# Attention scores by phases of three pairs of banks, with whole projections in between

## The chip, the cores and the metric

The kernel runs on one core of a Trainium2 chip. The metric is the device time of one execution in microseconds (us). A core has five engines that run their own instruction streams and meet through semaphores: TensorE (PE in the profile, its weight loads PEld), VectorE (DVE), ScalarE (ACT), GpSimd (POOL) and SyncE (SP, which here only issues DMAs). Matmul results lie in PSUM, which has eight banks of 128 partitions by 512 f32.

## The reference

A decoder layer over four sequences (B = 4) of 1024 tokens with 512 features, all in f32, with 16 heads of 32:

```
x = x + attn(layernorm(x))              # gated self-attention
x = x + xattn(layernorm(x), ctx)        # cross-attention, keys and values from ctx (384 features)
x = x + ffn(layernorm(x))               # 64 small networks with 16 hidden units each

attn:  a = softmax(inner @ outer.T / sqrt(32)) * aperture[q] * expression[k]
       a = a / (a.sum(-1) + 1e-8);  out = rotate(a @ v) @ Wout
xattn: out = softmax(q @ k.T / sqrt(32)) @ v @ Wo + bo
```

The two gates are sigmoids of small projections of x. The rotation of the heads is folded into the output weights.

## The kernel before, in words

**Units.** A unit is one of the two blocks (`ph` 0: self-attention, the first block; `ph` 1: cross-attention and the networks, the second) for one sequence; `order` has eight of them, first block first. Each unit has two halves (`hf`) of 512 queries. `attention(u, hf)` makes the list of 32 steps of a half unit: four groups `g` of four heads, and in each group eight key tiles `kt` of 128 keys.

**A step.** `scores(g, kt)` (L597 to L630) computes the scores of four heads, keys on partitions, queries on columns. It does so in two pairs `i` of two heads `j`. Each pair has a tile `s` of two PSUM banks, from a pool of two such tiles. Head `2 * i + j` has its queries and keys on 32 partitions of its own, so its matmul uses 32 rows of the array, and 64 of its columns (L608):

```
r = slice((2 * i + j) * DH, (2 * i + j + 1) * DH)
for m in range(0, P, 64):
    nc.tensor.matmul(s[m : m + 64, j, :],
        lhsT=k[r, g, kt * P + m : kt * P + m + 64], rhs=q[r, g, :], ...)
```

ScalarE takes the exponential of a pair in one instruction of 128x1024 (L613) into a tile `e`; six such tiles rotate. The denominators need sums of `e` over all keys. VectorE adds up the tiles of a pair in `es` (L619 at the second key tile, L621 after), for both pairs in most of the second block, and for the first pair alone where `shared` is set (the first block and the last unit); there the second pair's sums are made by TensorE (L643). In the first block VectorE also sums the first pair times the expression gate in `eg` (L628 for the first product, L629 for the rest). `es` and `eg` have tiles of their own.

**Times values.** `finish` of a step is held in `late` and issued one step later, after that step's scores. It multiplies `e` with the values into the accumulator `av` (L635), four heads side by side in four column tiles of 128 rows by 32 columns. At the last key tile `normalize` copies `av` and `sm` (L652, L654), and `after(steps, f)` puts the rest off by so many steps: `add_up` sums `es` and `eg` over partitions (L665) and sends the sums through DRAM (SyncE), `divide` forms reciprocals (L702), `multiply` makes the normalized result over the queries (L715).

**What goes beside.** `beside(u, hf)` lists all other work of a half unit in order: layernorm, transposes and projections of the unit to come (`pre`), and output projection, residual, layernorm and networks of the half before (`post`). Each part carries a load; a projection has three or four parts of load 1, each of which issues four column matmuls with `columns` (L87) over one chunk of 128 features. `run` hands parts out after every step in proportion to the load, so a projection can be spread over some steps while its bank stays open. `bank()` gives these banks, from a pool of two; another two hold `av` and `sm`. With the four banks of `s` that makes eight. Banks are emptied by ScalarE in most cases (`evacuate`, L281 and L283), by VectorE for values of the first block (L537) and for the output projections (L804).

**Order.** All engines' instructions stay in the order in which the program writes them. There is no planner; the order above is all there is.

**Roots.** A layernorm takes mean and variance on VectorE, then `rsqrt` (L289 to L301) on VectorE: an integer estimate and three Newton steps, twelve instructions on 128x4, and then `normalized` (L304). Only the very first half tile has its roots on GpSimd, as an addition and a power with the column `power` of -0.5 (L406, L407). GpSimd otherwise adds a bias (L812), copies marks (L829) and issues a few DMAs.

Of the kernel before, what the change touches and what calls it, by code (L numbers as in the profile page):

```python
# [16 lines left out]
P = 128  # L17
# [46 lines left out]
def moderate_path(tc: tile.TileContext, a: dict, out: bass.AP, flag: bass.AP):  # L64
    nc = tc.nc
    x = a["x"]
    with ExitStack() as st:
# [10 lines left out]
        p4 = enter(tc.tile_pool(name="mp4", bufs=4))  # L78

        def bank():  # L80
            return pf.tile([P, HALF], F32, tag="f", name="f")

        def columns(to, lhsT, rhs, **flags):
# [205 lines left out]
        def rsqrt(mv, n):  # L289
            ve = p2.tile([P, n], F32, tag="ve", name="ve")  # L290
            nc.vector.tensor_scalar(ve, mv[:, :, 1], EPS, None, ALU.add)
            yi = p2.tile([P, n], I32, tag="yi", name="yi")
            nc.vector.tensor_scalar(yi, ve.bitcast(I32), 1, None, ALU.logical_shift_right)
            nc.vector.tensor_scalar(yi, yi, -1.0, float(MAGIC), ALU.mult, ALU.add)
            y = yi.bitcast(F32)
            w = p2.tile([P, n], F32, tag="nw", name="nw")
            for _ in range(3):
                nc.vector.scalar_tensor_tensor(w, y, -0.5, y, ALU.mult, ALU.mult)
                nc.vector.tensor_tensor(w, w, ve, ALU.mult)
                nc.vector.scalar_tensor_tensor(y, w, 1.5, y, ALU.add, ALU.mult)  # L300
            return y  # L301
# [55 lines left out]
        def pre(u):  # L357
# [87 lines left out]
            def proj(what, g, hf):  # L445
# [3 lines left out]
                def part(cs):  # L449
                    def f():  # L450
                        if cs[0] == 0:
                            if "w" + what not in me:
                                fetch(what)
                            me["pj"] = bank()
                        for c in cs:
                            columns(
                                me["pj"], me["w" + what][:, c, ts(g, P)], me[kind, hf](c),
                                start=(c == 0), stop=(c == n - 1),
                            )
                        if cs[-1] == n - 1:  # L460
                            copy(me["pj"])
                    return len(cs), f
# [51 lines left out]
            def values(kt):  # L514
# [5 lines left out]
                def part(cs):  # L520
                    def f():
                        if cs[0] == 0:
                            if kt == 0:
                                if "wv" not in me:
                                    fetch("v")
                                me["v"] = p2.tile([P, NT, H, DH], F32, tag="v", name="v")
                            me["pv"] = bank()
                        for c in cs:
                            columns(
                                me["pv"], me[kind, hf, "t"](c, t), me["wv"][:, c, :],  # L530
                                start=(c == 0), stop=(c == n - 1),
                            )
# [52 lines left out]
        def attention(u, hf):  # L585
# [13 lines left out]

            def scores(g, kt):  # L600
                q, k = me["q", hf], me["k"]
                es = []
                for i in range(2):
                    s = ps.tile([P, 2, HALF], F32, tag="s", name="s")
                    for j in range(2):
                        r = slice((2 * i + j) * DH, (2 * i + j + 1) * DH)
                        for m in range(0, P, 64):
                            nc.tensor.matmul(  # L608
                                s[m : m + 64, j, :], lhsT=k[r, g, kt * P + m : kt * P + m + 64], rhs=q[r, g, :],
                                start=True, stop=True,  # L610
                            )
                    e = p4.tile([P, 2, HALF], F32, tag="e", name="e", bufs=6)
                    nc.scalar.activation(e, s, AF.Exp, scale=SCALE)  # L613
                    es.append(e)
                me["e", kt] = es
                for i in range(1 if shared and not closing(g) else 2):
                    if kt == 1:
                        me.setdefault("es", {})[i] = p1.tile([P, 2, HALF], F32, tag=f"es{i}", name="es")
                        nc.vector.tensor_tensor(me["es"][i], me["e", 0][i], es[i], ALU.add)  # L619
                    elif kt > 1:  # L620
                        nc.vector.tensor_tensor(me["es"][i], me["es"][i], es[i], ALU.add)  # L621
                if ph == 0 and kt > 0:
                    if kt == 1:
                        me["eg"] = p1.tile([P, 2, HALF], F32, tag="es1", name="eg")
                    for h in range(2):
                        eg, gate = me["eg"][:, h, :], lambda t: me["sw"][:, t, HG * g + h, 1:2]
                        if kt == 1:
                            nc.vector.tensor_scalar(eg, me["e", 0][0][:, h, :], gate(0), None, ALU.mult)  # L628
                        nc.vector.scalar_tensor_tensor(eg, es[0][:, h, :], gate(kt), eg, ALU.mult, ALU.add)  # L629
                return es  # L630

            def times(g, kt, es):
# [6 lines left out]
                if shared and kt % 2 and not closing(g):  # L639

                    for j in range(4):
                        t, h = kt - 1 + j // 2, j % 2
                        nc.tensor.matmul(  # L643
                            sm[j * DH : j * DH + sums, :],
                            lhsT=me["sw"][:, t, HG * g + 2 + h, :] if ph == 0 else ones, rhs=me["e", t][1][:, h, :],
                            start=(kt == 1), stop=(kt == NT - 1),
                        )

            def normalize(g):
# [3 lines left out]
                if shared:  # L653
                    nc.scalar.copy(both[:, 1, :], sm)  # L654
                    added = [me["es"][0][:, 0, :], me["es"][0][:, 1, :]]
                    if ph == 0:
                        added += [me["eg"][:, 0, :], me["eg"][:, 1, :]]
                else:
                    added = [me["es"][h // 2][:, h % 2, :] for h in range(HG)]
                after(1, lambda: add_up(g, i, both, added), behind=True)  # L660
# [56 lines left out]

            def step(g, kt):
                def f():
                    issue_due(False)  # L720
                    es = scores(g, kt)
                    issue_due(True)
                    if late:
                        late.pop(0)()
                    late.append(lambda: finish(g, kt, es))
                    tick[0] += 1
                return f

            def finish(g, kt, es):
# [3 lines left out]

            for g in range(HG):
                for kt in range(NT):
                    steps.append(step(g, kt))
            return steps

        def settle(u, hf, g):
# [5 lines left out]
            def sums():  # L745
                for j in range(HG):
                    nc.tensor.matmul(
                        sm[j * DH : (j + 1) * DH, :], lhsT=ones.to_broadcast([P, DH]), rhs=me["es"][j // 2][:, j % 2, :],
                        start=True, stop=True,
# [12 lines left out]
        def post(u, hf):  # L762
# [24 lines left out]
            def project(t):  # L787
                def part(cs, to=None):
                    def f():
                        assert last or me["divided", hf] >= cs[-1]  # L790
                        if cs[0] == 0:
                            res["po"] = to() if to else bank()
                            res["po", t] = res["po"]
                        if last:
                            res["po"] = res["po", t]
# [29 lines left out]

            def root(a=0, n=4):
                if ph == 1:
                    i = 2 * NS + b * NT + 4 * hf + a
                    nc.gpsimd.tensor_copy(marks[:, i : i + n], res["mv"][:, a : a + n, 1])  # L829
                rs = rsqrt(res["mv"][:, a : a + n, :], n)  # L830
                for t in range(n):
# [134 lines left out]

        def run(main, items):

            parts = sum(items, [])
            total = sum(c for c, _ in parts)  # L970
            done = 0
            for n, f in enumerate(main):
                f()
                while parts and (done + parts[0][0] / 2 <= total * (n + 1) / len(main) or n == len(main) - 1):
                    c, f1 = parts.pop(0)
                    if f1:
                        f1()
                    done += c

        def pause(load):  # L980
# [20 lines left out]
        def beside(u, hf):  # L1001
# [3 lines left out]
            if u + 1 == n:  # L1005
                h, out = held[0]["h"], last["wo"] + last["load"]
                k = min(len(h), 6)
                if hf:
                    ending.append(post(u, 1))
                    out += ending[0]["wo"]  # L1010
                out += pause(2) + weave(h[0:k], pause(10)) + weave(h[k:], last["o"]) + held.pop()["out"]
                out += (ending[0]["load"] if hf else []) + weave(last["ln"], pause(5)) + last["xT"]
# [65 lines left out]
        first += p["v"][1][0:3] + pres[1]["tr"][0] + p["v"][1][3:]  # L1078
        run([lambda: None], first)
        for u in range(n):  # L1080
            if u == 0:
                crossing.append(True)
            for hf in range(2):
                run(attention(u, hf), beside(u, hf))
        tail = ending[0]
        sums, divide, look = settle(n - 1, 1, HG - 1)
        late.pop(0)()

# [675 lines left out]
```

## Time and profile before

| what | value |
|---|---|
| median of three runs | 2196.32 us (2192.43 to 2196.33) |
| the profiled execution | 2195.77 us |
| its span, first to last instruction | 2193.9 us |
| granted TensorE clock, mean | 0.997 |
| TensorE busy | 2168.4 us (99%), 22750 matmuls |
| VectorE busy | 1558.3 us (71%) |
| ScalarE busy | 1240.3 us (57%) |
| GpSimd busy | 85.3 us (4%) |
| DMA, mean | 74 GB/s |

The page of the profile gives busy times, the chain of work that ended last, and groups of instructions: line, engine, operation, output and inputs, shapes and count, then busy time and mean of one in ns, then the idle time before them and who ended it. Each f32 matmul of the program is two in the profile, since the array passes over the columns twice. Matmuls run side by side in tiles of the array, so their single durations (0.6 us) add up to more than their busy time. A timeline row has start, duration, engine, line, operation, tiles, shape and count, and in brackets the idle time before it with its releaser.

Before the first scores, at 99.4 us, the kernel prepares the first unit; the last scores start at 2136.3 us, and the tail after them ends at 2193.9.

### The profile page before, as it was taken

To read this page: it belongs to the slowest core of one execution; us is meant where nothing else is said; L and a number is where in the kernel's file an instruction comes from. 1 tells how busy PE (TensorE), PEld (TensorE's weight loads), DVE (VectorE), ACT (ScalarE), POOL (GpSimd) and SP (SyncE) were. 2 spreads that over 40 slices of the span, in tenths; PEclk is the share of its full clock that TensorE was granted. 3 is DMA by queue.
4 is the path that set the end of the run, shared out by engine and by line. 5 is a ranking of instruction groups with operands and counts; after the bars stand their busy time and mean duration, and the time that the engine had idled before them with its cause. 6 is when DMAs were issued, how large, how long until landed. Compare 5 with 4: busy or idle time off the path is not lost.

```text
span 2193.9 us, 53076 instructions
## 1 busy us (share of the span) xinstructions
PE 2168.4 (99%) x22750; PEld 557.5 (25%) x22750; DVE 1558.3 (71%) x2510; ACT 1240.3 (57%) x1493; POOL 85.3 (4%) x127
## 2 busy tenths in 40 slices
PE   9999999999999999999999999999999999999996
PEld 4322222222222222222222222222222222222223
DVE  4578675796757957577686676877777777856477
ACT  0155545555455554555656566675757666577673
POOL 2000000030300000000000000000000000000000
PEclk9999999999999999999999999999999999999998
DMA  6312133032330221211222132221223142203131
GB/s 170 117 47 72 56 97 105 19 89 66 101 113 19 85 66 51 84 37 42 69 85 94 41 93 65 79 82 48 68 89 108 50 103 69 81 20 85 54 89 41
DMA packets 154137, 161.72 MB, mean 74 GB/s; under 512 B 47002, under 2 KB 92698, under 8 KB 152740
## 3 DMA queue, kind: packets, MB, share of 16 engines
q1 hardware_dynamic: 149828, 156.14, 24.7%
q8 instruction: 180, 2.95, 0.6%
q0 software_dynamic: 2080, 0.98, 0.3%
q10 hardware_dynamic: 1984, 1.12, 0.2%
q14 instruction: 65, 0.53, 0.1%
HBM read 115.40 MB, written 42.74 MB: 72 GB/s over the span
## 4 chain that ended last, share of the span: by engine, by line
PE 94%; DVE 2%; ACT 1%; issue 1%; DMA 1%; SPq 0%; POOL 0%; DVEq 0%; ACTq 0%
PE f L87 36%; PE s L608 25%; PE av L635 21%; PE sm L643 6%; PE sm L665 3%; ACT e L613 1%; DVE es L621 1%; PE f L913 1%; PE f L875 1%; PE s L87 1%; DVE g L902 1%; DMA xin<-in_x 0%; PE f L483 0%; PE s L913 0%; ACT hid L896 0%
## 5 line engine op out<-in xcount | busy, mean ns | idle before, releaser
L613 ACT ACTIVATE e<-s 128x1024 f32<-128x1024 f32 x1024 | 993.7, 1022 | 709.5 <-PE s L608 511.9
L621 DVE TENSOR_TENSOR es<-es,e 128x1024 f32<-128x1024 f32 x534 | 642.4, 1227 | 266.0 <-ACT e L613 264.2
L608 PE MATMUL s<-q,k 32*64 32x512 f32 x8192 | 607.3, 613 | 2.4 <-ACT e L613 0.8
L635 PE MATMUL av<-e,v 128*32 128x512 f32 x4096 | 550.2, 603 | 0.0
L87 PE MATMUL f<-xT,w 128*32 128x512 f32 x2816 | 333.7, 592 | 0.0
L629 DVE SCALAR_TENSOR_TENSOR eg<-e,sw,eg 128x512 f32<-128x512 f32 x448 | 318.4, 746 | 2.3
L619 DVE TENSOR_TENSOR es<-e 128x1024 f32<-128x1024 f32 x89 | 106.7, 1223 | 220.3 <-ACT e L613 188.4
L608 PEld LDWEIGHTS s<-q,k 32*64 32x64 f32 x8192 | 132.8, 129 | 446.2 <-ACT e L613 241.8
L87 PE MATMUL f<-w,q 128*32 128x512 f32 x1984 | 240.3, 592 | 0.0
L635 PEld LDWEIGHTS av<-e,v 128*32 128x32 f32 x4096 | 87.9, 108 | 403.9 <-issue 401.3
L87 PEld LDWEIGHTS f<-xT,w 128*32 128x32 f32 x2816 | 92.1, 110 | 210.5 <-issue 206.0
L643 PE MATMUL sm<-e,sw 128*2 128x512 f32 x1024 | 133.3, 592 | 0.0
L87 PE MATMUL f<-w,xT 128*32 128x512 f32 x896 | 106.0, 592 | 0.6 <-DVE q L285 0.6
L87 PEld LDWEIGHTS f<-w,q 128*32 128x32 f32 x1984 | 65.5, 110 | 149.1 <-issue 142.6
L87 PE MATMUL f<-w,ctxT 128*32 128x512 f32 x768 | 92.6, 592 | 0.0
L896 ACT ACTIVATE hid<-sT,units 128x256 f32<-128x256 f32 x128 | 76.5, 605 | 28.5 <-DVE g L902 24.1
L87 PE MATMUL f<-ctxT,w 128*32 128x512 f32 x768 | 92.3, 592 | 0.0
L812 POOL TENSOR_TENSOR r<-res,bo_bc 128x512 f32<-128x512 f32 x32 | 40.9, 1278 | 1041.5 <-DVE res L804 790.9
L902 DVE SCALAR_TENSOR_TENSOR g<-hid,units,g 128x256 f32<-128x256 f32 x120 | 57.5, 479 | 14.2 <-ACT hid L896 9.1
L665 PE MATMUL sm<-es,fixed 128*1 128x512 f32 x348 | 65.0, 591 | 0.0
L804 DVE TENSOR_TENSOR res<-f,res 128x512 f32<-128x512 f32 x62 | 42.5, 685 | 14.9 <-PE f L87 11.1
L715 DVE TENSOR_TENSOR q<-both,recb 128x512 f32<-128x512 f32 x63 | 43.2, 685 | 7.0 <-DMA recb<-rec_d 7.0
(265 smaller groups left out, 1046.2 us busy)
## 6 DMA issues: line engine op xcount, KB each, us to landing
recb<-rec_d SPq DMA_DIRECT2D x252, 64.0 KB
xT<-rows_d SPq DMA_DIRECT2D x60, 256.0 KB
rows_d<-r SPq DMA_DIRECT2D x60, 256.0 KB
w<-in_xattn_Wo SPq DMA_DIRECT2D x9, 1024.0 KB
w<-wout_d SPq DMA_DIRECT2D x8, 1024.0 KB
res<-in_x SPq DMA_DIRECT2D x32, 256.0 KB
x1b_d<-r SPq DMA_DIRECT2D x32, 256.0 KB
res<-x1b_d SPq DMA_DIRECT2D x32, 256.0 KB
```

The lines of the kernel that those rows point to most:

```text
L87: nc.tensor.matmul(to[r], lhsT=lhsT[:, j, :] if len(lhsT.shape) == 3 else lhsT[:, r], rhs=rhs, **flags)
L608: nc.tensor.matmul(s[m : m + 64, j, :], lhsT=k[r, g, kt * P + m : kt * P + m + 64], rhs=q[r, g, :], start=True, stop=True,)
L613: nc.scalar.activation(e, s, AF.Exp, scale=SCALE)
L619: nc.vector.tensor_tensor(me["es"][i], me["e", 0][i], es[i], ALU.add)
L621: nc.vector.tensor_tensor(me["es"][i], me["es"][i], es[i], ALU.add)
L629: nc.vector.scalar_tensor_tensor(eg, es[0][:, h, :], gate(kt), eg, ALU.mult, ALU.add)
L635: nc.tensor.matmul(av[r, :], lhsT=me["v"][:, kt, HG * g + h, :], rhs=es[h // 2][:, h % 2, :], start=(kt == 0), stop=(kt == NT - 1),)
L643: nc.tensor.matmul(sm[j * DH : j * DH + sums, :], lhsT=me["sw"][:, t, HG * g + 2 + h, :] if ph == 0 else ones, rhs=me["e", t][1][:, h, :], ...
L665: nc.tensor.matmul(sm[j * DH : j * DH + 1, :], lhsT=ones, rhs=e, start=True, stop=True)
L715: nc.vector.tensor_tensor(me["q", hf][:, g, :], both[:, 0, :], all_, ALU.mult)
L896: nc.scalar.activation(hid, res["s"], AF.Relu, bias=units[:, 1, h : h + 1], scale=units[:, 0, h : h + 1])
L902: nc.vector.scalar_tensor_tensor(res["g"], res["hid"], units[:, 2, h - 1 : h], res["g"], ALU.mult, ALU.add)
```

## The change

**Phases.** Steps are replaced by phases. `attention` now returns all 64 pairs (group, key tile, pair) of a half unit and a function `phase(size, early)`. `run_phases` takes three pairs, or two where a projection's bank is open (`keep` counts those), and whatever is left at the end. A phase first issues the score matmuls of all its pairs. The first two in issue order get the two tiles `s`; the third gets two banks from `bank()`, the pool of the projections. Where a part with load is due behind the phase, the pairs are issued in the order second, third, first, so that the pair whose exponential comes first sits in the projection banks. The exponential of the pair in separate banks is two instructions of 128x512 instead of one of 128x1024.

**What lies between.** After the scores come the times-values of all steps whose second pair was in the phase before, and then the parts that are due. Once a projection has begun, all its parts follow before the next phase. Where the phase before held the end of one group and the first step of the next, the end is issued after the first exponential, and the rest behind the projections. The clock of `after` advances by half a step a pair.

**Tiles.** `es` and `eg` now come from the pool of the `e` tiles, which has eight instead of six places; they are kept by group.

**Engines.** The first gated product goes from VectorE to ScalarE. `rsqrt` becomes two GpSimd instructions, an addition and a power, and the copy of marks is issued after the root. Two pauses in the plan of the last unit have other lengths.

```diff
+        def keep(first, last):
+            open_[0] += bool(first) - bool(last)
...
         def rsqrt(mv, n):
-            ve = p2.tile([P, n], F32, tag="ve", name="ve")
-            nc.vector.tensor_scalar(ve, mv[:, :, 1], EPS, None, ALU.add)
...
-            for _ in range(3):
-                nc.vector.scalar_tensor_tensor(w, y, -0.5, y, ALU.mult, ALU.mult)
-                nc.vector.tensor_tensor(w, w, ve, ALU.mult)
-                nc.vector.scalar_tensor_tensor(y, w, 1.5, y, ALU.add, ALU.mult)
+            y = p2.tile([P, n], F32, tag="yi", name="rs")
+            nc.gpsimd.tensor_scalar(y, mv[:, :, 1], EPS, None, ALU.add)
+            nc.gpsimd.tensor_tensor(y, y, power.to_broadcast([P, n]), ALU.pow)
             return y
...
+            def wide():
+                return p4.tile([P, 2, HALF], F32, tag="e", name="e", bufs=8)
+
+            def exponentials(g, kt, i, two, whole):
+                e = wide()
+                if whole is not None:
+                    nc.scalar.activation(e, whole, AF.Exp, scale=SCALE)
+                else:
                     for j in range(2):
+                        nc.scalar.activation(e[:, j, :], two[j], AF.Exp, scale=SCALE)
...
                         if kt == 1:
-                            nc.vector.tensor_scalar(eg, me["e", 0][0][:, h, :], gate(0), None, ALU.mult)
+                            nc.scalar.activation(eg, e0[0][:, h, :], AF.Identity, scale=gate(0))
...
+            pairs = [(g, kt, i) for g in range(HG) for kt in range(NT) for i in range(2)]
+
+            def phase(size, early):
+
+                issue_due(False)
+                mine, pairs[:] = pairs[:size], pairs[size:]
+                front = early and size == 3
+                order_ = [1, 2, 0] if front else range(len(mine))
+                places = {}
+                for n, j in enumerate(order_):
+                    whole = ps.tile([P, 2, HALF], F32, tag="s", name="s") if n < 2 else None
+                    two = [bank(), bank()] if whole is None else [whole[:, m, :] for m in range(2)]
+                    multiply_into(*mine[j], two)
+                    places[j] = (two, whole)
+                border = len(late) > 1 and late[0][0] == NT - 1
+                for n, pair in enumerate(mine):
+                    exponentials(*pair, *places[n])
+                    add(*pair)
+                    if n == 0 and border:
+                        issue_due(True)
+                        late.pop(0)[1]()
+                issue_due(True)
+                while late and not border:
+                    late.pop(0)[1]()
...
+                tick[0] += size / 2
+                return lambda: [f() for _, f in now]
...
+            while pairs:
+                size = min(len(pairs), 2 if open_[0] else 3)
+                upto = total * (all_ - len(pairs) + size) / all_
...
+                others = phase(size, early)
+                while parts and (open_[0] or due(parts[0][0], done)):
                     c, f1 = parts.pop(0)
                     if f1:
                         f1()
                     done += c
+                others()
```

## The prediction

> **What bounds the kernel.** I read the page first (busy shares, chain, groups), then TensorE's timeline of one step, then the weight loads of the same step, last the single records of all 512 score sets.
>
> ```profile
> span 2193.9 us, 53076 instructions
> ...
> PE 2168.4 (99%) x22750; PEld 557.5 (25%) x22750; DVE 1558.3 (71%) x2510; ACT 1240.3 (57%) x1493; POOL 85.3 (4%) x127
> ...
> PE f L87 36%; PE s L608 25%; PE av L635 21%; PE sm L643 6%; PE sm L665 3%; ACT e L613 1%; DVE es L621 1%; PE f L913 1%; PE f L875 1%; PE s L87 1%; DVE g L902 1%; DMA xin<-in_x 0%; PE f L483 0%; PE s L913 0%; ACT hid L896 0%
> ...
> L613 ACT ACTIVATE e<-s 128x1024 f32<-128x1024 f32 x1024 | 993.7, 1022 | 709.5 <-PE s L608 511.9
> L608 PE MATMUL s<-q,k 32*64 32x512 f32 x8192 | 607.3, 613 | 2.4 <-ACT e L613 0.8
> ```
>
> TensorE is the bound: 99% busy, over nine tenths of the chain, and 2.4 us of idle time before all score matmuls together. ScalarE (57%) and VectorE (71%) have room on average. So the price of the change is what it does to TensorE's sequence; work moved between the others counts only where it makes TensorE wait.
>
> What one step of (group, key tile) looks like on TensorE, and its weight loads:
>
> ```profile
> 1004.90 1.11 PE L608 MATMUL s<-q,k 32*64 32x512 f32 x16
> 1005.94 1.06 PE L635 MATMUL av<-e,v 128*32 128x512 f32 x8
> 1006.83 1.90 PE L87 MATMUL f<-w,ctxT 128*32 128x512 f32 x16
> 1008.65 1.11 PE L608 MATMUL s<-q,k 32*64 32x512 f32 x16
> ```
>
> ```profile
> 1006.83 0.13 PEld L87 LDWEIGHTS f<-w,ctxT 128*32 128x32 f32 x4 [0.30 <-issue]
> 1007.26 0.13 PEld L87 LDWEIGHTS f<-w,ctxT 128*32 128x32 f32 x4 [0.30 <-issue]
> 1007.68 0.13 PEld L87 LDWEIGHTS f<-w,ctxT 128*32 128x32 f32 x4 [0.30 <-issue]
> 1008.65 0.23 PEld L608 LDWEIGHTS s<-q,k 32*64 32x64 f32 x16 [0.84 <-ACT e L613]
> ```
>
> The reader is to see two things. A burst of four 128x32 matmuls follows the next at 0.43 us (1006.83, 1007.26, 1007.68): that is one pass of 512 f32 columns, and every matmul has two. And the sixteen of a score set, eight tiles of 32x64 (four heads' rows by two column halves) with two passes each, take 1.04 us from 1004.90 to 1005.94: also two passes, so **eight row tiles run side by side for the price of four column tiles**. The single records agree: first passes of all eight start within 47 ns, the second 0.480 us later, and 0.564 us after that the next burst starts.
>
> Against 2 x 0.429 a set so loses 0.187 us, the last burst ahead of it 0.113 (0.542 instead of 0.429), the first times-values burst behind it 0.024: **0.32 us for each trip into row tiles and back.** Over all 512 sets the records give 571.65 us from a set's start to the next burst (mean 1.117, because in 77 sets the two pairs start apart) and a lead of 0.112 each. One of the 77:
>
> ```profile
> 100.56 1.94 ACT L613 ACTIVATE e<-s 128x1024 f32<-128x1024 f32 x2 [15.82 <-PE s L608]
> ...
> 101.63 0.21 PEld L608 LDWEIGHTS s<-q,k 32*64 32x64 f32 x8 [1.03 <-ACT e L613]
> 101.63 2.00 PE L608 MATMUL s<-q,k 32*64 32x512 f32 x16
> 102.55 0.21 PEld L608 LDWEIGHTS s<-q,k 32*64 32x64 f32 x8 [0.71 <-ACT e L613]
> ```
>
> Each pair waits here for its own exponential to leave the bank. The first pair is alone in the array, and its passes are still 0.480 apart, and the second follows at the same pace: a pair alone is not faster than two together.
>
> **Part 1, three pairs in a phase.** A half unit has 64 pairs (4 groups, 8 key tiles, 2). Every projection that has been begun is finished before the next phase, so no bank is open when a phase is sized: 21 phases of three and one of one, 22 for 32 steps, over 16 half units 336 + 16 = 352 trips instead of 512.
>
> Removed: 160 trips' lead and first-burst loss, 160 x (0.112 + 0.024) = 21.7 us.
>
> Added: pairs alternate between heads 0/1 (upper rows) and heads 2/3 (lower rows). Three in a row hold two pairs of the same rows, in either issue order; two run together, the third has to follow on rows that were just in use, with the other half of the array empty. A phase costs 0.480 + 0.429 (the third's first pass) + 0.429 + 0.538 (from a four-tile pass to the next burst, as measured in the 77) = 1.876 us; if the third's passes are again 0.480 apart, 1.927. I take 1.90. A single pair: 0.480 + 0.538 = 1.018. So 336 x 1.90 + 16 x 1.018 = 654.7 us against 571.65: **+83.0 us, and with the trips saved +61.3 us** (53 to 70 by the two ends).
>
> A rule of the Trainium skill speaks for a higher price: "TensorE: Matmul & The Clock Gate", Part 3 (The mechanism, What overlaps and what doesn't), has weight loads overlap with running matmuls only where their row group differs. The third pair's loads have the row group of the first, so both of its passes would wait for some 0.13 us of loading: 336 x 2 x 0.13 = 87 us more, +148 instead of +61. The row above speaks otherwise: the loads of 1006.83 use all 128 rows, those of the matmuls then running, and cost the 0.43 us pitch nothing. I go by the row.
>
> **Part 2, the third pair's banks and whole projections.** The third pair takes both banks that projections rotate through; its exponential becomes two of 128x512. No such row exists; the nearest is the copy of that shape (L652 below, 0.591), so 2 x 0.59 - 1.02 = 0.16 us more, 54 us on ScalarE in all, beside TensorE work. What matters is the ends. After a projection's last pass the next burst comes at 0.54 and the third pair of the next phase 0.91 later, at 1.45. The bank is free after the pass (0.59), a hand-over and 0.69 of VectorE (L804, L537), some 1.35: hidden by 0.1 us, if the evacuating engine is idle. With ScalarE it is: three exponentials end about 5.2 us into a phase of 6.8 to 7.4 us (1.90 + 0.14 + times-values 1.29 + extra sums 0.64 in the first block + projection 3.43). With VectorE it isn't always: in the first block a phase with two upper pairs has 2 x (1.23 + 2 x 0.75) = 5.5 us of additions that start at about 3.1, and so end near 8.6, 1.1 us late. Some 52 of the 84 VectorE-evacuated projections lie there, half of them behind such a phase: 26 x 1.0 = 26 us; the other 58 at 0.15 make 9. **About +35 us.**
>
> In phases without a projection (228 projections for 352 phases, so 120 or more), the last exponential ends near 4.4 and the next third pair wants its bank at 4.2 (second block) to 4.9 (first): +5 us.
>
> **Part 3, e, es and eg in one pool of eight.** At the end of a group the old sums (held until they are added up, two phases on) and the new ones take four of eight, and three exponentials want places while three wait for times-values. Exponentials then wait until TensorE has passed its scores (1.9) and the first values (0.86), 1 to 1.7 us later than otherwise. Where a projection lies behind, that is covered; in about a quarter to a third of 64 group ends it is not: 64 x 0.25 = +16 us. Bounds: 0 to 64 x 1.5 = 96.
>
> **Part 4, roots and the first gated product.** The rows:
>
> ```profile
> L407 POOL TENSOR_TENSOR rs<-rs,fixed 128x1 f32<-128x1 f32 x4 | 2.4, 606 | 0.3
> L406 POOL TENSOR_SCALAR rs<-bnmv 128x1 f32<-128x1 f32 x4 | 1.3, 337 | 7.0 <-DVE bnmv L403 7.0
> ...
> L652 ACT COPY both<-av 128x512 f32<-128x512 f32 x63 | 37.3, 591 | 0.0
> L283 ACT ACTIVATE k<-f,bqk 128x512 f32<-128x512 f32 x32 | 22.0, 688 | 12.0 <-PE f L87 11.7
> L628 DVE TENSOR_SCALAR eg<-e,sw 128x512 f32<-128x512 f32 x64 | 30.7, 480 | 0.0
> L298 DVE SCALAR_TENSOR_TENSOR nw<-yi 128x4 f32<-128x4 f32 x66 | 10.7, 162 | 2.3
> ```
>
> A root of 12 small VectorE operations (0.23 + 0.17 + 0.18 + 9 x 0.162 = 2.0 us; 24 of them, 49 us) becomes 0.34 + 0.61 on GpSimd with two hand-overs, some 1.3 us, during which VectorE, in order, stands at the first normalization. "GPSIMD Engine Reference" (introduction) calls GpSimd the wrong engine for elementwise work, VectorE being about twice as fast: by that, 4 us a root and 24 x 2 = 48 us later on VectorE. The rows have two operations for twelve; I take 1.3. What is queued ahead on GpSimd is at most one addition of 1.28 us (L812) in the first block, which makes such a root as long as before, or DMA issues of the networks (0.6 us each), which run before or after, not between. All of this is VectorE time under TensorE's cover except in the tail, where two roots stand in the chain: -2 us. If the cover were gone, 24 roots could save 17 us. The first gated product, 64 x 0.48 us on VectorE, goes to ScalarE at about 0.69 (L283, the same shape with a per-partition operand), 44 us; both engines hide it: 0.
>
> **The sum.** 2195.8 (profiled execution: span 2193.9 and 1.9 around it; the median of the runs, 2196.3, is 0.5 above) + 61.3 + 35 + 5 + 16 - 2 = 2311; **forecast 2310 us**, a ratio of 0.951.
>
> **Rivals.** *The waits of parts 2 and 3 don't come* (evacuations and places are in time): 2195.8 + 61 - 2 = 2255. For it: before, VectorE at 88% in some half units (111 of 126 us) makes TensorE wait for nothing. *The waits pile up*, a late VectorE holding banks and places at once: with 1 us in every group end (64), 1.1 behind all 84 projections (92) and the rest as above, 2195.8 + 61 + 64 + 92 + 3 = 2415; I hold it between 2345 and 2415. Against: VectorE is given 80 us less work. *Faster, by one mechanism:* the third pair costs less than its two passes because half the array is free to be filled with it. If it cost in proportion to its tiles (0.43 us), 336 x 1.475 + 16.3 - 571.7 - 21.7 = -82 us, with the waits 2170. It decides at 336 x (1.045 + x) + 16.3 = 593.4, x = 0.67 us without waits, 0.50 with them. Against it stands the pace of single pairs in the 77 sets, 0.480 again. *Phases stay at two pairs*, some bank being always open: 2200 to 2235, as nothing is saved and projections are lumped; the loop that finishes open projections speaks against it.
>
> **Chances.** Forecast case (2285 to 2345) 0.50; no waits (2245 to 2285) 0.24; piled up 0.18; faster 0.06; two pairs 0.02. The range 2250 to 2375 leaves out the last two, a few of the second and about half of the third, some 2 in 10. A measurement of this kernel tells 0.2% (4.4 us) from no change: faster 0.06, same 0.01, slower 0.93.
>
> **What would show it.** Right: bursts of 24 score matmuls lasting 1.88 to 1.93 us, some 352 of them, eight starting together and four 0.9 later; score time on TensorE up by about 60 us net of the trips; new idle time before score and projection matmuls, put down to VectorE. Wrong: sets of 24 shorter than 1.7 us (the third pair finds room) or longer than 2.1 (loads exposed); VectorE-named waits absent; L608 bursts of 16 throughout.

## The result

The changed kernel takes 2450.22 us (median; 2441.25 to 2452.48) against 2195.37: a ratio of 1.1156 with a 95% interval of 1.1125 to 1.1187. The forecast was 2310 us (a ratio of 1.052 counted the same way), 2250 to 2375. The sign was right, the size wrong: +255 us where +115 were worked out.

The page of the changed kernel, with the rows that answer to those of before (the score matmuls now have two rows, `s` for the tiles of their own and `f` for the projection banks):

```profile
span 2450.7 us, 52959 instructions
...
PE 2347.7 (96%) x22750; PEld 661.2 (27%) x22750; DVE 1485.0 (61%) x2158; ACT 1300.5 (53%) x1893; POOL 119.6 (5%) x175
...
L615 ACT ACTIVATE e<-s 128x1024 f32<-128x1024 f32 x688 | 673.7, 1031 | 201.8 <-PE s L604 122.0
L618 ACT ACTIVATE e<-f 128x512 f32<-128x512 f32 x672 | 369.9, 599 | 530.8 <-PE f L604 405.8
...
L604 PE MATMUL f<-q,k 32*64 32x512 f32 x2688 | 408.7, 598 | 25.0 <-DVE res L831 8.5
L604 PE MATMUL s<-q,k 32*64 32x512 f32 x5504 | 419.9, 618 | 3.1 <-ACT e L615 1.4
```

The same 22750 matmuls. The two rows of score matmuls add up to 828.6 us, but run side by side in part: together they are busy in 765 us of the span, where it was 607.3. That is most of the difference, and TensorE is still the bound.

A phase that nothing disturbs looks as it was worked out. TensorE's timeline of the changed kernel:

```profile
1005.96 1.11 PE L604 MATMUL s<-q,k 32*64 32x512 f32 x16
1006.90 1.04 PE L604 MATMUL f<-q,k 32*64 32x512 f32 x8
1007.87 1.92 PE L643 MATMUL av<-e,v 128*32 128x512 f32 x16
1009.61 1.04 PE L651 MATMUL sm<-e,sw 128*2 128x512 f32 x8
1010.46 3.62 PE L92 MATMUL f<-xT,w 128*32 128x512 f32 x32
```

Two pairs start at 1005.96, the third at 1006.90 when their passes are through, and times-values at 1007.87: 1.91 us for three pairs. The median of all 336 such sets is 1.903 us.

From the starts of single matmuls, before and after, I divide the 256.8 us by which the span grew (lost to half clock means: half of the time in which the granted clock was 0.5):

| where TensorE's time went | before, us | after, us | difference |
|---|---|---|---|
| score sets, undisturbed price (after: 336 x 1.90 + 16 x 1.018) | 571.6 in all | 654.7 | +83.1 |
| score sets, waits of the third pair, and some of the second | in the above | 105.1 | +105.1 |
| score sets, half clock | 0.0 | 12.8 | +12.8 |
| lead of a set, over 0.429 us | 57.1 | 38.0 | -19.1 |
| between sets, half clock | 0.0 | 31.6 | +31.6 |
| between sets, waits and the rest | 1409.4 | 1456.0 | +46.6 |
| head and tail | 155.8 | 152.4 | -3.4 |

Three terms are not those of the forecast: 105 us of waits in the score sets (35 and 5 were put down), 44 us of half clock (none) and 35 of the last 47 us, which one line explains. Another 10 us lie before the first matmuls of the networks (L902), which wait for VectorE's transposes. TensorE's waits in the changed kernel, with total, count and longest:

```profile
PE sm L651 <- ACT both L674: 35.4, 18, 2.6
PE f L902 <- DVE xn L316: 10.3, 3, 4.0
PE f L604 <- DVE res L831: 8.5, 2, 7.8
PE f L604 <- DVE v L536: 5.5, 5, 1.7
PE sm L673 <- ACT both L662: 4.2, 2, 2.1
```

**The wait for the sums' bank.** TensorE's timeline at a border between two groups, then ScalarE's:

```profile
779.25 1.04 PE L673 MATMUL sm<-e,fixed 128*1 128x512 f32 x8
780.11 1.04 PE L643 MATMUL av<-e,v 128*32 128x512 f32 x8
783.77 1.77 PE L651 MATMUL sm<-e,sw 128*2 128x512 f32 x8 [2.63 <-ACT both L674]
```

```profile
780.32 1.08 ACT L618 ACTIVATE e<-f 128x512 f32<-128x512 f32 x2 [2.52 <-PE sm L673]
781.29 1.95 ACT L615 ACTIVATE e<-s 128x1024 f32<-128x1024 f32 x2
783.10 0.62 ACT L674 COPY both<-sm 128x512 f32<-128x512 f32 x1
```

The partition sums (L673) are through at 780.3, but their copy (L674) was written behind the three exponentials of the phase and starts at 783.10. The next group's sums (L651) need that bank and are due right after the first burst of times-values: TensorE stands for 2.63 us. Sixteen such waits of 1.8 to 2.6 us lie at two group borders in each of the eight half units of the first block.

**The half clock.** Busy time and granted clock (PEclk) in the stretch up to the end of that wait, and in the two behind it:

```profile
780.00:783.90 3.90, 1.27 (x16) 0.23 (x12) 1.54 (x2) 3.40 (x5) 0.00 (x0) 1.00 0.00 0
783.90:787.30 3.40, 3.40 (x25) 0.76 (x21) 2.29 (x5) 0.00 (x0) 0.00 (x0) 0.51 0.05 10
787.30:790.00 2.70, 2.70 (x32) 0.67 (x24) 0.31 (x2) 1.41 (x3) 0.00 (x0) 0.99 0.19 18
```

For 3.4 us after the wait TensorE has half its clock: the two bursts of L651 take 1.77 us instead of 1.04. Within the span such stretches add up to 100 us after the change and to 12 before, where all of them lie in the tail.

**The third pair's banks.** TensorE's timeline of one phase that asks for a bank which VectorE has yet to empty, then VectorE's:

```profile
114.11 1.11 PE L604 MATMUL s<-q,k 32*64 32x512 f32 x16
115.04 1.02 PE L604 MATMUL f<-q,k 32*64 32x512 f32 x4
117.36 1.07 PE L604 MATMUL f<-q,k 32*64 32x512 f32 x4 [1.30 <-DVE w L208]
```

```profile
114.17 1.22 DVE L630 TENSOR_TENSOR e<-e 128x1024 f32<-128x1024 f32 x1
115.30 1.40 DVE L638 SCALAR_TENSOR_TENSOR e<-e,sw 128x512 f32<-128x512 f32 x2
116.63 0.68 DVE L208 COPY w<-f 128x512 f32<-128x512 f32 x1
```

The first head of the third pair has its bank and runs alone, x4, in a quarter of the array; the second starts 2.32 us after it, and the set takes 4.26 us instead of 1.90. VectorE first makes three additions and products, then empties the bank.

A second head that comes late **costs its delay and hardly more**. By the starts of single matmuls there are 59 sets, without half clock, in which it alone is late, by 0.17 to 2.7 us: they are longer by that delay and at most 0.08 us, 0.04 at the median. Where it comes during the first head's passes, it still runs beside the rest of them: 14 sets in which it is 0.17 to 0.43 us late are 0.22 to 0.43 us longer.

In about 100 of 336 third pairs the second head starts after the first, in 73 of them by more than 0.1 us. By the operation that ended the last wait in a set, with half clock taken off, the sets are longer by 53 us in 38 sets behind banks that VectorE empties, by 31 us in some 35 behind banks that ScalarE empties, and by 16 us in 29 with the exponential of the third pair before as the last wait. In 21 of these 29 (8 us) it is the second pair that makes the set longer: it waits for the exponential in its own tile, and the third pair then follows it at the usual distance.

Of VectorE's 53 us, 16 lie behind additions to the outputs of the networks (L946), and 6 in a single set, in which VectorE itself waits for a DMA before it can empty the bank:

```profile
1259.94 0.69 DVE L831 TENSOR_TENSOR res<-f,res 128x512 f32<-128x512 f32 x1 [12.29 <-DMA res<-in_x]
```

ScalarE is late because more than exponentials stands in its queue. TensorE's timeline of one such phase, then ScalarE's:

```profile
1753.73 1.11 PE L604 MATMUL s<-q,k 32*64 32x512 f32 x16
1754.66 1.98 PE L604 MATMUL f<-q,k 32*64 32x512 f32 x8
```

```profile
1754.45 0.60 ACT L923 ACTIVATE hid<-sT,units 128x256 f32<-128x256 f32 x1 [0.78 <-DVE g L929]
1754.95 0.56 ACT L286 COPY v<-f 128x512 f32<-128x512 f32 x1
```

The copy that empties the bank stands behind an activation of the networks (L923), which waits for VectorE. So it is in 20 sets (15 us); in 10 it stands behind the copies of a group's end (L660, L662; 9 us), in 6 behind an exponential (7 us).

### The profile page after: what moved, and what is told of

It reads as the page before. It is cut to its first block, busy times and chain, and to the rows that moved or that the text cites. A ratio compares the mean times of both kernels' runs of the same rounds, so it can differ in the third digit from the quotient of the medians.

```text
span 2450.7 us, 52959 instructions
## 1 busy us (share of the span) xinstructions
PE 2347.7 (96%) x22750; PEld 661.2 (27%) x22750; DVE 1485.0 (61%) x2158; ACT 1300.5 (53%) x1893; POOL 119.6 (5%) x175
## 4 chain that ended last, share of the span: by engine, by line
PE 81%; ACT 5%; DVE 4%; issue 2%; DMA 1%; SPq 1%; POOL 0%; DVEq 0%; ACTq 0%
PE f L92 28%; PE av L643 17%; PE s L604 14%; PE f L604 13%; PE sm L651 5%; ACT e L615 3%; PE sm L673 2%; DVE e L630 1%; ACT e L618 1%; PE f L902 1%; DVE e L638 1%; PE f L940 1%; DMA rows_d<-r 0%; DVE g L929 0%; DMA rec_d<-rec 0%
## 5 line engine op out<-in xcount | busy, mean ns | idle before, releaser
L630 DVE TENSOR_TENSOR e<-e 128x1024 f32<-128x1024 f32 x534 | 638.7, 1224 | 495.2 <-ACT e L615 279.4
L615 ACT ACTIVATE e<-s 128x1024 f32<-128x1024 f32 x688 | 673.7, 1031 | 201.8 <-PE s L604 122.0
L618 ACT ACTIVATE e<-f 128x512 f32<-128x512 f32 x672 | 369.9, 599 | 530.8 <-PE f L604 405.8
L604 PE MATMUL f<-q,k 32*64 32x512 f32 x2688 | 408.7, 598 | 25.0 <-DVE res L831 8.5
L604 PE MATMUL s<-q,k 32*64 32x512 f32 x5504 | 419.9, 618 | 3.1 <-ACT e L615 1.4
L92 PE MATMUL f<-xT,w 128*32 128x512 f32 x2816 | 318.2, 593 | 0.7 <-ACT e L618 0.7
L638 DVE SCALAR_TENSOR_TENSOR e<-e,sw 128x512 f32<-128x512 f32 x448 | 315.4, 745 | 2.9 <-ACT e L637 2.7
L628 DVE TENSOR_TENSOR e<-e 128x1024 f32<-128x1024 f32 x89 | 108.5, 1225 | 236.8 <-ACT e L615 147.9
L643 PEld LDWEIGHTS av<-e,v 128*32 128x32 f32 x4096 | 104.9, 110 | 386.9 <-issue 369.7
L604 PEld LDWEIGHTS f<-q,k 32*64 32x64 f32 x2688 | 127.7, 132 | 241.7 <-issue 119.8
L604 PEld LDWEIGHTS s<-q,k 32*64 32x64 f32 x5504 | 91.1, 130 | 309.4 <-issue 181.1
L651 PE MATMUL sm<-e,sw 128*2 128x512 f32 x1024 | 137.2, 608 | 33.1 <-ACT both L674 33.1
L923 ACT ACTIVATE hid<-sT,units 128x256 f32<-128x256 f32 x128 | 76.7, 611 | 36.9 <-DVE g L929 35.9
```

Source lines behind the costliest of these rows:

```text
L92: nc.tensor.matmul(to[r], lhsT=lhsT[:, j, :] if len(lhsT.shape) == 3 else lhsT[:, r], rhs=rhs, **flags)
L604: nc.tensor.matmul(two[j][m : m + 64], lhsT=k[r, g, kt * P + m : kt * P + m + 64], rhs=q[r, g, :], start=True, stop=True,)
L615: nc.scalar.activation(e, whole, AF.Exp, scale=SCALE)
L618: nc.scalar.activation(e[:, j, :], two[j], AF.Exp, scale=SCALE)
L628: nc.vector.tensor_tensor(me["es", g][i], e0[i], e[i], ALU.add)
L630: nc.vector.tensor_tensor(me["es", g][i], me["es", g][i], e[i], ALU.add)
```

## The experiments

**Moved operations alone.** The kernel before, with roots on GpSimd and the first product on ScalarE:

```diff
-            nc.vector.tensor_scalar(ve, mv[:, :, 1], EPS, None, ALU.add)
...
+            nc.gpsimd.tensor_scalar(y, mv[:, :, 1], EPS, None, ALU.add)
+            nc.gpsimd.tensor_tensor(y, y, power.to_broadcast([P, n]), ALU.pow)
...
-                            nc.vector.tensor_scalar(eg, me["e", 0][0][:, h, :], gate(0), None, ALU.mult)
+                            nc.scalar.activation(eg, me["e", 0][0][:, h, :], AF.Identity, scale=gate(0))
```

> The kernel before with nothing but the moved operations: roots as a power on GpSimd, marks copied after the root, first gated product on ScalarE. Theory (both lie beside TensorE work, the tail gains about 2 us): 2188 to 2196 us. Rival (VectorE stands still behind GpSimd's roots and holds banks): 2210 us or more.

Measured: 2191.07 us, a ratio of 0.9981 (0.9973 to 0.9989). The stretch between first and last scores is as before (2038.9 against 2038.2 us), the tail is 5.6 us shorter (50.8 against 56.4). So this part costs nothing in the kernel before and gains 0.2%; it is the only version here that is faster than both kernels. What the moved operations cost inside the phases, where ScalarE's queue matters more, was not tried by itself. A root isn't as cheap as forecast:

```profile
L292 POOL TENSOR_TENSOR rs<-rs,fixed 128x4 f32<-128x4 f32 (+1 forms) x24 | 26.5, 1105 | 2.0
L399 POOL TENSOR_TENSOR rs<-rs,fixed 128x1 f32<-128x1 f32 x4 | 2.4, 610 | 0.3
```

The power grows with its elements: 1.1 us in the mean of 22 on 128x4 and two on 128x2, 0.61 on 128x1, which the forecast took for all.

**Two pairs in a phase.**

```diff
-                size = min(len(pairs), 2 if open_[0] else 3)
+                size = min(len(pairs), 2)
```

> The changed kernel with phases of two pairs at most; whole projections, the common pool of eight tiles, the GpSimd roots and the ScalarE product stay. Theory (the third pair is what costs: its two passes on a half-empty array, 80 us net of nothing, its waits for projection banks, 109 us, and the half clock behind long waits): 512 sets of about 1.05 us again, no score matmul in projection banks, 2190 to 2230 us. Rival (whole projections, the common pool or the moved operations cost most of the 255 us): 2300 us or more.

Measured: 2339.21 us (1.0654; 1.0636 to 1.0672). The theory that only the third pair costs is clearly missed, and the rival's range is hit; which of its three parts it is, the next run tells. TensorE's timeline of this kernel at a phase without a projection, then ScalarE's:

```profile
1416.60 1.07 PE L643 MATMUL av<-e,v 128*32 128x512 f32 x8
1417.79 2.00 PE L604 MATMUL s<-q,k 32*64 32x512 f32 x16
1419.72 1.06 PE L643 MATMUL av<-e,v 128*32 128x512 f32 x8
```

```profile
1416.71 1.94 ACT L615 ACTIVATE e<-s 128x1024 f32<-128x1024 f32 x2 [0.33 <-PE s L604]
1418.94 1.94 ACT L615 ACTIVATE e<-s 128x1024 f32<-128x1024 f32 x2 [0.29 <-PE s L604]
```

Between two score sets lies one burst of times-values, so both pairs of 1417.79 wait for the exponentials that began at 1416.71 and come one after the other: 1.93 us for the set instead of 1.04. Score sets take 698.7 us (571.6 before), their lead 79.7 (57.1). Whole projections leave such bare phases; single parts, as before, fill each step.

**Two pairs, projections by parts again.**

```diff
-                while parts and (open_[0] or due(parts[0][0], done)):
+                while parts and (done + parts[0][0] / 2 <= upto or not pairs):
```

> As the run with two pairs, and projections handed out by single parts in proportion again, so that their banks stay open over phases; the common pool of eight, the GpSimd roots and the ScalarE product stay. Theory (what the two-pair run lost, 144 us, comes from projections in lumps: phases without one leave TensorE 2.0 to 2.5 us of work against 2.0 us of exponentials and their hand-overs, so that its first pairs wait): 2185 to 2200 us, as the run with the moved operations alone. Rival (the common pool of e, es and eg holds places back): 2240 us or more.

Measured: 2210.05 us (1.0064; 1.0047 to 1.0080), so 129 of the 144 us above the kernel before went with the lumps: of the rival's three parts it was whole projections. The time is 10 us above what was expected, below the 2240 of the pool as a rival, and 19 above the run with the moved operations. The common pool and the phase form lie between these two runs; 8 us of the difference are in the score sets, and which of the two makes it stays open.

**The sums' copy earlier.** The changed kernel with:

```diff
-                    if n == 0 and border:
+                    if n == 0:
                         issue_due(True)
-                        late.pop(0)[1]()
-                issue_due(True)
+                        if border:
+                            late.pop(0)[1]()
```

> The changed kernel, but what is due behind the scores (the sums over partitions and their copy out of the sums' bank, above all) is issued after the first exponential of a phase and not after the last. Theory (the 35 us in which TensorE waits for the copy of line 674 are made by three exponentials queued ahead of that copy): that wait falls below 8 us, some half-clock time goes with it, 2395 to 2420 us. Rival (the copy is late because its sums are late): within 10 us of the changed kernel.

Measured: 2410.50 us (1.0977; 1.0959 to 1.0995), 39.7 us less. The wait as this kernel's trace has it:

```profile
PE sm L651 <- ACT both L674: 4.0, 5, 0.8
```

31 us of waiting are gone, and the loss by half clock falls from 50 to 40 us. The cause of this term is shown: the place of the copy in ScalarE's queue.

**VectorE's banks emptied by ScalarE.** The changed kernel with a ScalarE copy out of the bank ahead of VectorE's work, at three places:

```diff
-                        nc.vector.tensor_tensor(r, res["po"], r, ALU.add)
+                        nc.vector.tensor_tensor(r, emptied(res["po"]), r, ALU.add)
...
-                    nc.vector.tensor_tensor(res[i], po[k], res[i], ALU.add)
+                    nc.vector.tensor_tensor(res[i], emptied(po[k]), res[i], ALU.add)
...
-                                nc.vector.tensor_tensor(me["v"][:, kt], pvh, ex, ALU.mult)
+                                nc.scalar.copy(me["v"][:, kt], pvh)
+                                nc.vector.tensor_tensor(me["v"][:, kt], me["v"][:, kt], ex, ALU.mult)
```

> The changed kernel, with the banks that VectorE emptied (first-block values, output projections, network outputs) first copied out by ScalarE, VectorE then adding or multiplying from SBUF. Theory (VectorE's queue of additions holds the third pair's banks: 53 of the 109 us of bank waits end with VectorE): those waits go, some by ScalarE take their place, 2385 to 2415 us. Rival (any emptying of a bank that a third pair wants next is late, whoever does it): within 12 us of the changed kernel.

Measured: 2407.06 us (1.0971; 1.0953 to 1.0990), 43 us less. Waits that end with VectorE fall from 53 to 5 us, but the new copies hold third pairs for 26 us, so that the waits in the sets give back only 24 us; another 24 come from the clock, whose loss falls from 50 to 26 us. The theory's range is hit and the rival's 12 us are not, but the rival has a part: VectorE is the worst holder, and a late emptying by ScalarE holds the third pair too.

**Both mends.** The changed kernel with the two edits above together.

> The changed kernel with both mends of the first runs, what is due issued after the first exponential and VectorE's banks emptied by ScalarE. Theory (they take away two separate waits, 40 and 43 us): 2360 to 2375 us; what stays above the kernel before is the third pair's passes (83 us, less 20 for the trips) and some 85 us of bank waits behind ScalarE. Rival (they take away the same wait): 2395 us or more.

Measured: 2357.88 us (1.0730; 1.0712 to 1.0748). 92 us are gone, more than the sum of the two (83) and 2 us past the expected range, and 14 us of clock loss are left. The rest above the kernel before has the undisturbed passes as its largest term (83 us), then 72 us of waits in the score sets.

**The price of a pair alone.** The kernel before, which issues the scores of the first pair, or of both, a second time into the same banks (`range(1)`, in the other run `range(2)`):

```diff
+                for i in range(1):
+                    for j in range(2):
+                        r = slice((2 * i + j) * DH, (2 * i + j + 1) * DH)
+                        for m in range(0, P, 64):
+                            nc.tensor.matmul(places[i][m : m + 64, j, :], ...)
```

> The kernel before, which issues the score matmuls of the first pair (upper rows) a second time into the same banks, before both exponentials; nothing else changes. Theory (a pair costs two full passes, whatever half of the array it leaves empty): 512 x 0.83 to 0.86 us, less some 35 us of waits that vanish in the longer steps: 2580 to 2635 us. Rival (a pair costs in proportion to its tiles, 0.43 us): 2380 to 2415 us.

> The kernel before, which issues the score matmuls of both pairs a second time. Theory (both together cost the same two passes as one alone): within 20 us of the run that repeats one pair. Rival (by tiles): 2600 to 2640 us with the other run at 2380 to 2415.

Measured: 2586.58 us for one pair (1.1777; 1.1754 to 1.1801) and 2625.50 for both (1.1954; 1.1930 to 1.1978). TensorE's timelines, one pair again first, both again after:

```profile
1200.47 1.11 PE L608 MATMUL s<-q,k 32*64 32x512 f32 x16
1201.38 1.04 PE L617 MATMUL s<-q,k 32*64 32x512 f32 x8
1202.34 1.06 PE L645 MATMUL av<-e,v 128*32 128x512 f32 x8
```

```profile
1221.09 1.11 PE L608 MATMUL s<-q,k 32*64 32x512 f32 x16
1222.00 1.06 PE L617 MATMUL s<-q,k 32*64 32x512 f32 x16
1222.99 1.07 PE L645 MATMUL av<-e,v 128*32 128x512 f32 x8
```

Eight matmuls more on half of the array or sixteen on all of it: 1.87 and 1.90 us (medians over 512 sets 1.876 and 1.903). One repeated pair costs +391 us, both +430. The first is inside its range. The runs are 39 us apart, not within 20: the score sets differ by 42 us, 14 by the 27 ns by which the usual set is longer and the rest by sets of the second run whose pairs start apart. A price by tiles would have made the runs some 220 us apart (512 x 0.43). So the third pair pays for two whole passes, 0.86 us, and leaves half of the array empty.

**Three pairs only where the banks are free.**

```diff
-                size = min(len(pairs), 2 if open_[0] else 3)
+                size = min(len(pairs), 2 if used[0] else 3)
+                used[0] = False
```

`used` is set by each projection part. This kernel leaves out one VectorE multiplication, the last of group 2 in the last half unit (0.69 us).

> The changed kernel, where a phase takes three pairs only if no projection has been issued since the phase before, and two otherwise; so a third pair never asks for a bank that a projection has just filled. Theory (the third pair's bank waits, 105 us with 13 us of half clock among them, come from the projection right ahead): split third pairs fall from 100 to below 25, score sets lose some 100 us, less what the additional trips (some 80 x 0.14 us) take, and the waits for the sums' bank (35 us) may stay: 2290 to 2350 us. Rival (the banks are held by the exponentials of the third pair before, or by anything else): split third pairs stay near 100 among fewer phases of three, 2400 us or more.

Measured: 2380.98 us (1.0844; 1.0825 to 1.0863), 69 less than the changed kernel but 30 above the range. Split third pairs fall from about 100 to 29 (from 73 to 22 by more than 0.1 us; below 25 of the 100 were expected), so it is mostly the projection right ahead that splits them. But 95 sets of three now wait for exponentials with their first pairs, some 50 us in all, as in the two-pair run: these phases follow phases without a projection, where TensorE has too little else to do. The part of it that shows as idle time of TensorE, in the changed kernel and here:

```profile
PE s L604 <- ACT e L615: 1.4, 1, 1.4
PE s L606 <- ACT e L617: 13.2, 27, 1.9
```

The waits moved. A repetition, which was to issue any times-values left over at the end:

> As the run before it (three pairs only where no projection was issued since the phase before), with the last key tile's times-values, which that one left out, issued again. The run before it had 2381 us, 30 to 90 above what was expected: its split third pairs fell from 100 to 29, but in 95 of its phases of three the first two pairs waited for their tiles' exponentials instead (52 us). So: 2375 to 2395 us, with the same two counts; 2350 or less would mean that the missing matmuls had moved something.

Measured: 2378.41 us (1.0848; 1.0823 to 1.0872). That is inside its range, and the counts are about the same (30 split third pairs). The expectation names the wrong omission: no times-values were missing in the run before it (4096 matmuls of `av` in both), and this kernel leaves out the same multiplication.

## Why the prediction was wrong

**Right.** The bound, the 352 trips and a phase's price. The median set took 1.903 us for 1.90, with some luck: 1.90 was the middle of two cases, and neither is the usual one. The third pair's two passes are 0.429 us apart, as in the lower case, but it starts 0.936 us into the set and not 0.909, which adds 27 ns; in some 40 sets it starts at 0.909, and they take 1.88.

The weight of the row against the rule was right as well. By the rule of the Trainium skill ("TensorE: Matmul & The Clock Gate", Part 3, What overlaps and what doesn't) the third pair's second pass would follow 0.13 us later than it does; it follows at 0.429 us, so its loads are hidden although they go to rows in use. The prediction read that part narrowly: under The mechanism it also lets a load go ahead of running matmuls when it targets the background weight buffer. Which of the two a load does, no run here shows.

The trips saved 19.1 us in leads alone; 21.7 were forecast for leads and first bursts. The moved operations are hidden and head and tail are 3.4 us shorter (the tail 5.6 in the run with them alone), for 2 forecast, though a root's power is 1.1 us and not 0.61. Together these terms give +61 (83.1 - 19.1 - 3.4), where +59 was forecast.

**Wrong, the step that decides: Part 2, the waits for the third pair's banks.** Its 35 + 5 us measured 105. Its way of pricing, a late bank at its delay, held. Three sizes did not:

- "With ScalarE it is" (that the evacuating engine is in time) put ScalarE's banks at nothing; they cost 31 us. The step counted three exponentials in ScalarE's queue and left out the activations of the networks and the copies of a group's end.
- VectorE's banks, put at 35 us, cost 53: 38 sets at 1.4 us, where 26 at 1.0 and 58 at 0.15 were put down. The banks of the networks' outputs (16 us) and the wait for a DMA (6 us) were not among the projections that it counted.
- In the phases without a projection, 16 us were lost for the 5 put down, half of them by the second pair, which the step let start with the first.

**Wrong, a term that was missing: the clock.** Before, TensorE was idle for at most 0.27 us at a time between the first scores and the last, and its clock was whole there. The new waits cost their own length and, in 17 cases, 1.7 us or a multiple more by the clock: 44 us. The runs with waits taken away lose less by it in step (50 us over the whole span of the changed kernel; 40, 26, 14 in the mended ones).

**Wrong, a place: Part 3.** It looked for the price of a group's end in the places of the common pool (16 us). The price was at the sums' bank, 35 us, by the order in ScalarE's queue, as the run with the earlier copy shows. The pool's own price, with that of the phase form, is at most the 19 us between two runs.

These three misses are 65, 44 and 19 us of the 140 us between forecast and result, and the waits before L902 add 10; why those transposes come later stays open. The rival "the waits pile up" had VectorE's late banks, but put 92 us on them for 53 measured, and had neither the clock nor ScalarE nor the sums' bank; its 2345 to 2415 lies below the result too.

**What the two-pair run adds.** I expected the third pair to be the whole cause. In fact the change makes two things depend on each other: a third pair needs projections to be whole, and whole projections leave bare phases. With two pairs these wait for exponentials (+144 us); with three that wait is small (some 10 us), but the third pair's empty half, banks and clock cost more. Neither half of the change pays for the other.

## What to carry to other kernels

Before saving mode switches, count passes: matmuls share a pass only if they lie in different tiles of the array, and a third pair needs tiles that one of the first two has, so an odd half set costs a whole one, here 0.86 us against 0.32 us for a trip. When a resource is shared between two streams, list everything in the queue of the engine that frees it, not only the work that the change is about: here the networks' activations and a group's copies made ScalarE late. And work that is lumped so that a bank is free leaves stretches elsewhere that are short of work; look what bounds those, and where a copy stands in its engine's queue.

## What the runs showed of the hardware

Between the first and the last scores of the changed kernel the granted clock fell to 0.5 in 17 stretches, each of 3.4 us or of two or three times that. In each case a wait of TensorE of 0.77 us or more lay in the 3.4 us before, or was running. Not every such wait has one: of 37 waits of 0.77 us or more 18 have none, among them waits of 2.6 and 2.9 us, and in the two-pair run five waits of 0.9 to 1.9 us have none. An engine that was busy for 96% of the span so lost 50 us by its clock alone. That the waits are the cause is argued from their order in time and from the runs in which both shrink together; it was not tried by itself.

Score matmuls on half of the array cost what those on all of it cost: eight more for a set +391 us over 512 sets, sixteen more +430. A head that starts during the passes of another runs beside the rest of them: 14 sets with one 0.17 to 0.43 us late were 0.22 to 0.43 us longer.

On GpSimd a power on 128x4 took about 1.1 us, on 128x2 0.73, on 128x1 0.61.
